# Four-layer graph network on one core: the last group's layers 2 and 3 in two pieces, activation tables loaded ahead, transposes between the last steps, and an order written out operation by operation

## The chip, the core and the metric

The kernel runs on one core of a Trainium2 chip. The engines named below are PE (TensorE, the matrix engine), DVE (VectorE), ACT (ScalarE), POOL (GpSimd) and SP (SyncE, which here only issues DMA transfers). Each engine works through its own list of instructions in the order in which the program put them; between engines, semaphores make an instruction wait until its inputs are there. The metric is the device time of one execution in microseconds (us), median of several runs. All data are float32.

## What is computed

The input is 128 small graphs of 64 nodes with 256 features each, and their adjacency matrices. Two graphs fill the 128 partitions, and such a pair is called a block, so there are 64 blocks. Four layers follow each other, each as `x = layernorm(x + layer(x))`:

```
# layer 0: five message-passing steps with a GRU cell
for l in range(5):
    agg = A^T @ (h @ weight[l]);  h = gru_cell(agg, h, w_ih, w_hh, b_ih, b_hh)
# layer 1: neighbour sum, 256 -> 1024 features, RMS norm, silu, 1024 -> 256
agg = eps * x + adj @ x;  h = silu(rmsnorm(agg @ W1 + b1) * rms_weight);  out = h @ W2 + b2
# layer 2: map to the tangent space, neighbour sum, back onto the ball
t = artanh(|x|) * x / |x|;  s = adj @ t;  out = project(tanh(|s|) * s / |s|)
# layer 3: attention over neighbours
h = x @ W_w^T + W_b;  u = adj * exp(e_i + f_j + a_b);  out = (u / sum(u)) @ h
```

A graph's rows never meet another graph's, so any set of blocks can be worked on alone.

## The kernel before, in words

The 64 blocks are cut into 16 groups of NB = 4 blocks (512 rows); `group(g)` (from L635) writes down all operations of one group, layers 0 to 3, as a *stream*. Layer 0 (`gated`, from L774) holds most of the matrix work. Layer 1's product into 1024 features is `by_sums` (the `p_ah`, `p_bh` and `p_ch` products of L1000, copied to `hid` by L334 or L335 and added up by L1005); the squares for the RMS norm are L986, their sum `ps_ss`, the factor `ps_rms`, the scaling L1049 and the silu L1051. The product back, `ps_o1` (32 matrix products of 256 columns for a group; the profile drops the digit and calls it `ps_o`), is the last large piece of matrix work of a group.

What follows is short work in a long chain, and it is done for the group's four blocks together. Sum onto the residual (L707), layer norm (`layer_norm`, L712 to L751: statistics L733 and L734 on DVE, a power on POOL L737, an offset L746, the scaled rows `x_n` by L339 on ACT or L340 on DVE), then layer 2: a row of tiny DVE operations on 128 x 4 values (L1090 to L1113), one of them a logarithm on ACT (L1098) and one a polynomial (`series`, L1101) that takes the logarithm's place where the norm is under `SERIES_BELOW`; the rows scaled (`tan`, L1117 or L1118), four products with the adjacency (`ps_sup`), squares with a sum on ACT (L1130), a square root on POOL (L1134), a tanh on ACT (L1139), six tiny DVE operations (`onto_ball`, L1142), the sum (L707) and a layer norm. Layer 3: eight transposes (`ps_T`, L668), copies to `x3T` (L334), eight products of 258 columns (`ps_a`), exponentials (L1189), scaled rows `hw` (L1192), four products with the adjacency (`ps_att`), a few tiny DVE operations (L1204 to L1207), the sum (L707), a layer norm and the output transfer (L1212).

Only the last two groups, 14 and 15, take this DVE form, the transposes by PE, and the statistics instructions (`summed` is false, `late` is true). The other fourteen do the tiny operations on POOL and the transposes by DVE and DMA.

ACT holds one set of function tables at a time. The logarithm, the silu and the exp are in three different sets (tanh is in the last two), and going from one to another takes an `ACT_TABLE_LOAD` in front of the function that needs it.

The order of the work on all engines is not the order in which the operations are written down. `Plan` (L54) goes through the streams with a cost model: at each step it takes, of the next few operations of each engine and up to four streams, the one that can start first, with ties settled by one of four rules; which rule holds in which stretch of 7 us is written in the string `CHOICES` (L156). It keeps eight PSUM banks, the DMA transfers and the ACT table in account. `issue` (L224) then gives out the operations in that order, and the order is kept on each engine.

```
    for g in range(NG):
        flow.stream()
        group(g)
    flow.issue()
```

Of the kernel before, what the change touches and what calls it, by code (L numbers as in the profile page):

```python
# [14 lines left out]
OP = mybir.AluOpType  # L15
# [7 lines left out]
SERIES_BELOW = 0.25  # L23
# [19 lines left out]
class Op:  # L43
    __slots__ = ("eng", "us", "run", "ways", "stream", "n", "kb", "sets", "need", "then", "bufs", "opens", "id", "way", "port")

    def __init__(self, ways, stream, n, kb, sets, port=()):
        self.port = port
        self.ways = {eng: (us, run) for eng, us, run in ways}
        self.eng, self.us, self.run = ways[0]
        self.stream, self.n, self.kb, self.sets = stream, n, kb, sets  # L50
        self.need, self.then, self.bufs, self.opens, self.id, self.way = 0, [], (), None, 0, 0.0


class Plan:  # L54


    def __init__(self, flow):
        self.flow = flow
        ops = [o for s in flow.streams for o in s]
        self.need = [o.need for o in ops]  # L60
        self.at = [0.0] * len(ops)
        self.uses = {}
        self.clock = dict.fromkeys(flow.AHEAD, 2.5)
        self.queues = [{e: deque(o for o in s if e in o.ways) for e in self.clock} for s in flow.streams]
        self.banks = [0.0] * BANKS
        self.left, self.first, self.bus = len(ops), 0, 0.0
        self.lands = [0.0] * flow.TRANSFERS
        self.order, self.table, self.port = [], None, 0.0

    def advance(self, until, rank):  # L70


        flow, need, at, clock, banks = self.flow, self.need, self.at, self.clock, self.banks
        while self.left and clock["PE"] < until:
            best = None
            for s in range(self.first, min(self.first + flow.WINDOW, len(self.queues))):
                for e, q in self.queues[s].items():
                    opened = False
                    for _, o in zip(range(flow.AHEAD[e]), q):
                        t = max(clock[e], at[o.id], self.port) if e in o.port else max(clock[e], at[o.id])  # L80
                        if o.opens is not None:
                            if opened or not banks or need[o.id]:
                                opened = True
                                continue
                            t = max(t, banks[0])
                        elif need[o.id]:
                            continue
                        elif o.kb and e != "POOL":
                            t = max(t, self.lands[0])
                        elif o.sets and self.table not in o.sets:  # L90
                            t += flow.TABLE
                        key = (t + flow.SOONER if len(o.ways) > 1 and e == "DVE" else t, *rank(s, o))
                        if best is None or key < best[0]:
                            best = key, o, e, t
            if best is None:
                return False
            _, o, eng, t = best
            if o.sets and self.table not in o.sets:
                self.table = o.sets[0]
            for e in o.ways:  # L100
                self.queues[o.stream][e].remove(o)
            self.order.append((eng, o))
            end = t + o.ways[eng][0]
            clock[eng] = end
            if eng in o.port:
                self.port = end
            if o.opens is not None:
                banks.pop(0)
            for b in o.bufs:
                n = self.uses.get(b, b.left) - 1  # L110
                self.uses[b] = n
                if not n:
                    banks.append(end + flow.hop(eng, "PE"))
                    banks.sort()
            if o.kb:
                self.bus = max(self.bus, end + flow.DMA[0]) + o.kb / flow.DMA[1]
                end = self.bus + flow.DMA[2]
                if o.eng != "POOL":
                    self.lands = [*self.lands[1:], end]
            for u in o.then:  # L120
                need[u.id] -= 1
                at[u.id] = max(at[u.id], end + flow.hop(eng, u.eng))
            self.left -= 1
            while self.first < len(self.queues) and not any(self.queues[self.first].values()):
                self.first += 1
        return True


class Flow:

    AHEAD = {"PE": 32, "DVE": 10, "ACT": 10, "POOL": 4, "SP": 2}


    HOPS = {"from PE": 0.22, "to PE": 0.42, "else": 0.06, "own": 0.0}

    REACH = {"from PE": 0.22, "to PE": 0.15, "else": 0.06, "own": 0.0}

    SOONER = 0.4


    DMA = (2.0, 330.0, 1.0)
    TRANSFERS = 8

    TABLE = 1.28
    WINDOW, STRETCH, LAGS = 4, 7.0, (60.0, 150.0)
    CHOICES = ("0010032202000010000101000000100101200211212021110210210022212000010021010211122100122212200010120021"  # L156
               "0210111100010100200111200121100102102211102100100010001002101010121001100100121112200201010102002100"
               "1010101001102000211100212100110100021110222020000101220210121200200010100201210100110111010011010111"
               "1000111101110110111001011000")
# [47 lines left out]
    def hop(self, e, to, hops=None):  # L207
        hops = hops or self.HOPS
        if e == to:
            return 0.0 if e == "PE" else hops["own"]  # L210
        return hops["from PE" if e == "PE" else "to PE" if to == "PE" else "else"]

    def ways(self):

        for i, o in enumerate(o for s in self.streams for o in s):
            o.id = i
        path = {}
        for ops in self.streams:
            longest = 0.0
            for o in reversed(ops):  # L220
                path[o] = o.us + max((path[u] + self.hop(o.eng, u.eng, self.REACH) for u in o.then if u.stream == o.stream), default=0.0)
                o.way = longest = max(longest, path[o])

    def issue(self):  # L224
        self.ways()
        ranks = (lambda s, o: (s, o.n), lambda s, o: (s if o.kb else -s, o.n), *(lambda s, o, lag=lag: (lag * s - o.way, s, o.n) for lag in self.LAGS))
        plan, until = Plan(self), 0.0
        for c in self.CHOICES:
            until += self.STRETCH
            assert plan.advance(until, ranks[int(c)])  # L230
        assert not plan.left
        last = {}
        for eng, o in plan.order:
            made = o.ways[eng][1]()
            for i in made if isinstance(made, list) else [made]:
                if eng in last:
                    self.tc.add_manual_dep(i.ins, last[eng].ins.name, self.BEHIND, reason="the plan's order")
                last[eng] = i
# [3 lines left out]
def kernel(  # L242
# [392 lines left out]
    def group(g):  # L635
        s = g % NF
        NB = SIZES[g]
# [74 lines left out]
        def layer_norm(y, st, tag, name, norm=None):  # L712
# [6 lines left out]
            def row(b):  # L719
                return [(y, b)]  # L720

            if summed:
                few_s((lambda: mv[:, :, 0], mv), lambda: st[:, :, 0], -1.0 / D, OP.mult, [st])
                for b in range(NB):
                    act(400, lambda b=b: nc.scalar.activation(
                        o[:, b, :], y[:, b, :], AF.Square, bias=mv[:, b, 0:1], accum_out=st[:, b, 1:2]),
# [4 lines left out]
            else:  # L731
                for b in range(NB):
                    dve(256, lambda b=b: nc.vector.bn_stats(st[:, b, :], y[:, b, :]), [(st, b)], row(b))  # L733
# [14 lines left out]
            for b in range(NB):  # L748
                scaled(256, lambda b=b: o[:, b, :], lambda b=b: y[:, b, :], lambda b=b: rstd[:, 0, b:b + 1],
# [3 lines left out]
        if g >= 2:  # L753
            load(g)
        xt, xs = loads.pop(g)
        ed = edge[s]
        ps = bank("ps_adjT")
        for b in range(NB):
            turn(lambda ps=ps, b=b: nc.tensor.transpose(ps[:, b * P:(b + 1) * P], ed[:, b, :], ident.tile()),
                 [ps], [ed])  # L760
        adjT = u("adjT", "adjT", (P, NB, P))
        copied(R, lambda: adjT.tile().rearrange("p b (m r) -> p b m r", m=Q),
               lambda ps=ps: ps[:, :R].rearrange("p (b r m) -> p b m r", b=NB, m=Q), [adjT], [ps])
        dve(R, lambda: nc.vector.tensor_scalar(ed[:, :NB, :], ed[:, :NB, :], 0.0, None, OP.not_equal), [ed], [ed])
        hT = u("h", "hT", (P, KD, R))
# [8 lines left out]
        def gated(l, h):  # L774
# [13 lines left out]
            def agg_of(n):  # L788
                aggregate(agg, hr, n, ed, l > 0)
# [460 lines left out]
```

## Time and profile before

| what | value |
|---|---|
| three runs | 2296.31, 2296.64 (median), 2298.32 us |
| the profiled execution: its own time | 2296.92 us |
| its span, first to last instruction | 2295.1 us |
| PE busy | 2245.7 us, 98% of the span |
| DVE, ACT, POOL busy | 1696.8 us (74%), 1308.8 us (57%), 554.3 us (24%) |
| mean granted PE clock | 0.994 of full speed |
| last `ps_o1` product of group 15 ends | 2252.08 us |
| last PE instruction ends | 2284.1 us |

Times inside the execution are counted from the first instruction. A float32 product runs on PE as two passes, so the profile counts two matmuls for each product that the kernel asks for; a transpose of 128 x 128 is one. "Idle" of an engine is the length of a stretch less its busy time in it.

### The profile page before, as it was taken

Reading aid. Unit: us, or ns where it says so; the run is one execution under the profiler, and the core shown is the slowest. Engines: PE = TensorE matmul, PEld = TensorE weight load, DVE = VectorE, ACT = ScalarE, POOL = GpSimd, SP = SyncE. Lnnn points to the kernel's source line nnn. Section 1 sums busy time; section 2 is a strip of 40 time slices with the busy share of each in tenths; the row PEclk is TensorE's granted clock in tenths of the full one; section 3 lists DMA queues with packets and bytes.
Section 4 is the critical chain, followed back from the end, with each engine's and each line's share of the span. In section 5 each row is a group of like instructions: output and inputs, shape, how many; then the busy total and the mean of one; then the engine's idle time right before and its main releaser. Section 6 shows DMA issues by size and latency. Waiting matters only on the chain.

```text
span 2295.1 us, 32440 instructions
## 1 busy us (share of the span) xinstructions
PE 2245.7 (98%) x11242; PEld 1979.1 (86%) x11242; DVE 1696.8 (74%) x3633; ACT 1308.8 (57%) x2800; POOL 554.3 (24%) x902
## 2 busy tenths in 40 slices
PE   9999999999999999999999999999999999999986
PEld 7888888888888888888888888888888888888774
DVE  5777867767777778677777777778777777777776
ACT  3344656675556556566566656556565665555564
POOL 2200222441122223132322223222231322112201
PEclk9999999999999999999999999999999999999998
DMA  5111112121212012121211212012122121211200
GB/s 146 33 23 33 28 19 58 19 49 29 48 28 47 22 28 58 19 45 33 36 42 25 52 28 47 21 29 49 28 49 37 22 53 21 49 19 20 46 10 19
DMA packets 428771, 84.21 MB, mean 37 GB/s; under 512 B 399124, under 2 KB 427824, under 8 KB 428608
## 3 DMA queue, kind: packets, MB, share of 16 engines
q1 hardware_dynamic: 426880, 80.26, 17.7%
q8 instruction: 89, 1.46, 0.3%
q10 hardware_dynamic: 1328, 1.31, 0.2%
q0 software_dynamic: 400, 0.57, 0.1%
q14 instruction: 74, 0.61, 0.1%
HBM read 32.55 MB, written 8.39 MB: 18 GB/s over the span
## 4 chain that ended last, share of the span: by engine, by line
PE 93%; DVE 3%; ACT 1%; POOL 1%; DMA 1%; issue 1%; SPq 0%; POOLq 0%; ACTq 0%; DVEq 0%
PE p_ga L817 23%; PE p_gc L817 12%; PE ps_o L316 9%; PE ps_agg L316 7%; PE p_ix L823 6%; PE p_gb L817 6%; PE p_hx L823 6%; PE p_ah L1000 4%; PE p_hy L823 4%; PE p_iy L823 4%; PE ps_a L316 2%; PE p_ch L1000 2%; PE ps_att L316 1%; PE ps_sup L316 1%; PE p_bh L1000 1%; PE ps_wmih L316 1%
## 5 line engine op out<-in xcount | busy, mean ns | idle before, releaser
L316 PE MATMUL ps_o<-w2s,hid 128*128 128x256 f32 x1024 | 230.9, 379 | 4.3 <-ACT hid L1051 4.3
L316 PEld LDWEIGHTS ps_o<-w2s,hid 128*128 128x128 f32 x1024 | 194.0, 190 | 31.7 <-ACT hid L1051 5.5
L351 POOL TENSOR_SCALAR mv<-st 128x4 f32<-128x4 f32 x56 | 15.6, 278 | 829.5 <-DVE y L707 442.0
L339 ACT ACTIVATE hnb<-p_hx,half_b 128x256 f32<-128x256 f32 x213 | 100.3, 471 | 143.0 <-PE p_hx L823 111.7
L817 PE MATMUL p_gc<-tA,w_h 128*128 128x256 f32 x640 | 173.2, 381 | 0.1
L817 PE MATMUL p_gc<-tB,w_a 128*128 128x256 f32 x640 | 172.3, 379 | 1.1 <-DVE tB L354 1.0
L817 PE MATMUL p_ga<-tA,w_h 128*128 128x256 f32 x640 | 171.7, 379 | 0.0
L817 PE MATMUL p_ga<-tB,w_a 128*128 128x256 f32 x640 | 168.4, 379 | 1.1 <-DVE tB L354 1.1
L817 PE MATMUL p_ga<-hT,w_h 128*128 128x256 f32 x640 | 168.3, 380 | 0.7 <-DVE U L867 0.4
L817 PE MATMUL p_ga<-agg,w_a 128*128 128x256 f32 x640 | 167.1, 379 | 0.0
L316 PEld LDWEIGHTS ps_agg<-edge,hr 128*128 128x128 f32 x1024 | 142.2, 193 | 12.4 <-DVE a_t L621 3.0
L316 PE MATMUL ps_agg<-edge,hr 128*128 128x128 f32 x1024 | 143.5, 276 | 2.8 <-DVE a_t L621 2.6
L870 ACT ACTIVATE U<-U,half_b 128x512 f32<-128x512 f32 (+1 forms) x160 | 94.0, 628 | 79.7 <-DVE U L867 79.6
L817 PEld LDWEIGHTS p_gc<-tB,w_a 128*128 128x128 f32 x640 | 121.0, 190 | 17.8 <-DVE tB L354 1.6
L817 PEld LDWEIGHTS p_ga<-tB,w_a 128*128 128x128 f32 x640 | 120.5, 190 | 18.1 <-DVE tB L354 1.8
L817 PEld LDWEIGHTS p_gc<-tA,w_h 128*128 128x128 f32 x640 | 121.2, 191 | 16.6 <-ACT V L334 0.5
L817 PEld LDWEIGHTS p_ga<-agg,w_a 128*128 128x128 f32 x640 | 119.7, 190 | 15.7 <-issue 0.5
L817 PEld LDWEIGHTS p_ga<-hT,w_h 128*128 128x128 f32 x640 | 118.5, 190 | 16.0 <-DVE U L867 0.8
L817 PEld LDWEIGHTS p_ga<-tA,w_h 128*128 128x128 f32 x640 | 117.9, 190 | 14.1
L334 ACT COPY agg<-ps_agg 128x512 f32<-128x512 f32 x140 | 81.0, 579 | 78.9 <-PE ps_agg L316 77.9
L870 ACT ACTIVATE V<-V,half_b 128x256 f32<-128x256 f32 (+1 forms) x160 | 87.8, 586 | 59.5 <-DVE V L867 58.9
L883 DVE TENSOR_TENSOR V<-p_ix,V 128x256 f32<-128x256 f32 x192 | 80.6, 420 | 35.3 <-PE p_ix L823 32.4
(285 smaller groups left out, 5667.1 us busy)
## 6 DMA issues: line engine op xcount, KB each, us to landing
hr<-t SPq DMA_DIRECT2D x256, 128.0 KB, 3.2
x<-in_x_dram SPq DMA_DIRECT2D x64, 128.0 KB, 2.7
xr<-in_x_dram SPq DMA_DIRECT2D x16, 512.0 KB, 4.3
out_dram<-x_n SPq DMA_DIRECT2D x16, 512.0 KB, 2.9
xs<-in_x_dram SPq DMA_DIRECT2D x120, 64.0 KB, 2.4
x3T<-t SPq DMA_DIRECT2D x56, 128.0 KB, 3.1
edge<-in_adj_dram SPq DMA_DIRECT2D x64, 32.0 KB, 2.2
wm<-in_L_gnn_weight_dram SPq DMA_DIRECT2D x5, 256.0 KB, 3.3
```

What stands on the lines that cost most here:

```text
L316: return nc.tensor.matmul(o, lhsT, rhs, start=(k == 0), stop=(k == nk - 1))
L334: flow.either([("ACT", 0.22 + 0.00077 * n, lambda: nc.scalar.copy(o(), i())), ("DVE", 0.145 + 0.00105 * n, lambda: nc.vector.tensor_copy(o ...
L339: flow.either([("ACT", 0.3 + 0.0008 * n, lambda: nc.scalar.activation(o(), i(), AF.Identity, bias=bias(), scale=scale())), ("DVE", 0.145 + ...
L351: pool(0.25, lambda: nc.gpsimd.tensor_scalar(w[0](), x(), s0, s1, op0, *((op1,) if op1 else ())), [w[1]], r)
L817: pe(HR, lambda i=i, w=w, c=c: nc.tensor.matmul(ps[:, c * HR:(c + 1) * HR], w[:, m, c * P:(c + 1) * P], v[i][0](), start=first and i == 1 ...
L823: pe(HR, lambda: nc.tensor.matmul(ps[:, j * HR:(j + 1) * HR], w[:, m, :], v[0](), start=first, stop=True, skip_group_check=True), [ps], [( ...
L870: act(HR if len(w) == 1 else R, lambda: nc.scalar.activation(o(), src(), AF.Tanh, bias=half_b[:, i * KD + c:i * KD + c + 1], scale=0.5), w ...
L883: dve(HR + 44, lambda: nc.vector.tensor_add(uu[:, c, half(n)], region(ps, j), uu[:, c, half(n)]), [(uu, (n, c))], [ps, (uu, (n, c))])
L1000: pe(HR, lambda c=c: nc.tensor.matmul(ps[:, c * HR:(c + 1) * HR], w1f[:, w, (2 * q + c) * P:(2 * q + c + 1) * P], v[0](), start=first and ...
```

## The change

1. **Last group in two pieces.** `group(g)` stops for g = 15 after layer 1 and returns `y1` and `adjT`. Two more streams then do layers 2 and 3 for two blocks each (`NB` = 2): piece 0 for blocks 0 and 1 in the buffers of slot 1, piece 1 for blocks 2 and 3 in those of slot 0. `layer_norm` gets the argument `at`, the first row block to read. Each piece has its own output transfer, so there are 611 transfers on SP's list for 610.
2. **Tables ahead.** In groups 14 and 15, `table` puts a one-operand `Ln` (before the chain of layer 2) and a one-operand `Tanh` (after it) on ACT. With this, ACT's list has six more small activations and 49 table loads for 47.
3. **Transposes between the steps.** In piece 1 only, `busy` puts 4 x 6 PE transposes into a bank that nobody reads, each six after one tiny result: `rn`, `n2`, `us` (shown as `ss`) and `urn` (shown as `rn`).
4. **Shorter polynomial.** `SERIES_BELOW` goes from 0.25 to 0.125, and the polynomial loses three of its seven terms, for all groups: 84 tiny POOL instructions less over groups 0 to 13, and three tiny DVE instructions less in each chain of groups 14 and 15.
5. **Order.** `Plan`, its cost model and `CHOICES` go. `placed` reads a string `ORDER` with one mark for each of the 13105 operations; a mark names the engine, the stream (of six) and the place in that engine's waiting list.

In the order that results, half of PE's products stand 10 or more places from where they stood, nine in ten within 43, counted among products of one kind and pair of tiles. On DVE, half stand 14 or more places away. The groups begin and end in the same sequence up to group 13. At the end it differs: before, the 32 `ps_o1` products of group 14 and the 32 of group 15 stand mixed together, and layer 2 of both groups stands behind them. After, group 14's `ps_o1` stand before group 15's first layer-1 product, and group 14's four `ps_sup` before group 15's `ps_o1`. Group 13's `ps_a` and `ps_att` stand among group 15's layer-1 products, where they stood about the start of group 15's fifth message-passing step. Behind group 15's last `ps_o1` stand group 14's `ps_T`, `ps_a` and `ps_att`, and the two pieces, piece 0 ahead of piece 1.

The core of the diff:

```
-SERIES_BELOW = 0.25
+SERIES_BELOW = 0.125
...
-    def issue(self):
-        self.ways()
...
-        for c in self.CHOICES:
-            until += self.STRETCH
-            assert plan.advance(until, ranks[int(c)])
...
+    def placed(self):
+        at, n = self.SIGNS.index, len(self.SIGNS)
+        waiting = [{e: [o for o in s if e in o.ways] for e in self.ENGINES} for s in self.streams]
+        first, marks = 0, iter(self.ORDER)
+        for c in marks:
+            i = at(next(marks)) * n + at(next(marks)) if c == "~" else at(c)
+            i, e = divmod(i, len(self.ENGINES))
+            i, s = divmod(i, self.AHEAD)
+            o, eng = waiting[first + s][self.ENGINES[e]][i], self.ENGINES[e]
...
+            yield eng, o
...
-    def group(g):
-        s = g % NF
-        NB = SIZES[g]
+    def group(g, piece=None):
+        s, NB, base = piece[:3] if piece else (g % NF, SIZES[g], 0)
...
+            if g == NG - 1:
+                return y1, adjT
+        else:
+            y1, adjT = piece[3:]
+            st1 = stats()
...
-        x2 = layer_norm(y1, st1, "A", "n1", xn)
+        x2 = layer_norm(y1, st1, "A", "n1", xn, base)
+        def table(func, sets, after):
+            if not summed:
+                act(4, lambda: nc.scalar.activation(warm, one4, func), [], [after], sets)
+        def busy(after, n=6):
+            if piece and base:
+                ps = bank("ps_warm")
+                for i in range(n):
+                    turn(lambda i=i: nc.tensor.transpose(
+                        ps[:, i % 4 * P:(i % 4 + 1) * P], after.tile()[:, :1].to_broadcast([P, P]), ident.tile()), [ps], [after])
+        table(AF.Ln, LN, xn)
...
+            busy(rn)
...
-                    v.scalar_tensor_tensor(ser.tile(), n2.tile(), 1.0 / 13.0, one4[:, :NB], OP.mult, OP.mult),
+                    v.scalar_tensor_tensor(ser.tile(), n2.tile(), 1.0 / 7.0, one4[:, :NB], OP.mult, OP.mult),
                     *(v.scalar_tensor_tensor(ser.tile(), ser.tile(), 1.0 / q, n2.tile(), OP.add, OP.mult)
-                      for q in (11, 9, 7, 5, 3)),
+                      for q in (5, 3)),
...
+            busy(n2)
...
+        table(AF.Tanh, TANH, fac)
...
+        busy(us)
...
+            busy(urn)
...
     for g in range(NG):
         flow.stream()
-        group(g)
+        made = group(g)
+        for i in range(2 if made else 0):
+            flow.stream()
+            group(g, ((g + 1 - i) % NF, SIZES[g] // 2, SIZES[g] // 2 * i, *made))
     flow.issue()
```

## The prediction

> **What bounds the kernel now.** I read the busy time by stretches first, then PE's waits near the end, then the chain of work that ended last, then PE's and ACT's instructions after the last `ps_o1`.
>
> The columns of the stretches are: from and to, length, busy time (instructions) of PE, PE's weight loads, DVE, ACT, POOL, then the granted PE clock, the DMA share and GB/s.
>
> ```profile
> 100.00:200.00 100.00, 100.00 (x512) 89.32 (x511) 77.70 (x150) 45.21 (x87) 0.00 (x0) 1.00 0.17 27
> 200.00:600.00 400.00, 395.94 (x1987) 350.55 (x1986) 294.75 (x623) 235.07 (x502) 104.15 (x176) 1.00 0.18 34
> 1400.00:1800.00 400.00, 399.44 (x2023) 355.06 (x2022) 304.59 (x637) 233.50 (x503) 102.23 (x164) 1.00 0.18 36
> ```
>
> ```profile
> 2100.00:2160.00 60.00, 55.95 (x275) 48.43 (x273) 44.55 (x90) 35.45 (x83) 18.58 (x42) 1.00 0.16 31
> 2160.00:2190.00 30.00, 28.82 (x138) 25.54 (x137) 19.67 (x57) 17.13 (x37) 5.16 (x6) 0.89 0.17 46
> 2190.00:2226.00 36.00, 28.53 (x136) 23.70 (x136) 30.54 (x58) 22.65 (x38) 4.39 (x3) 0.95 0.00 0
> 2226.00:2252.10 26.10, 26.07 (x127) 22.72 (x125) 14.27 (x49) 10.91 (x18) 2.64 (x2) 1.00 0.00 1
> 2252.10:2269.20 17.10, 5.61 (x16) 3.89 (x16) 12.14 (x60) 10.14 (x32) 4.62 (x4) 0.82 0.00 0
> 2269.20:2284.10 14.90, 14.86 (x64) 11.73 (x64) 11.66 (x42) 10.72 (x26) 2.68 (x2) 0.86 0.00 0
> 2284.10:2295.10 11.00, 0.02 (x1) 0.00 (x0) 5.16 (x21) 3.16 (x6) 1.19 (x2) 0.63 0.27 95
> ```
>
> From 100 to 2100 us PE is full: the idle of the stretches adds up to 7.5 us in 2000 (0 to 100 us has 6.7 more). No order can win more there than this idle. The end is another case: 12.7 us of idle from 2100 to 2252.1, then 43.0 us in which PE has some 20 us of work. PE's waits from 2100 us on name the causes (total, times, longest):
>
> ```profile
> PE ps_T L668 <- ACT x_n L339: 5.9, 1, 5.9
> PE ps_sup L316 <- DVE tan L1118: 5.3, 1, 5.3
> PE p_hy L823 <- DVE y L707: 3.7, 1, 3.7
> PE p_ah L1000 <- DVE hid L1005: 2.7, 1, 2.7
> ```
>
> And the PE and ACT instructions behind `ps_o1`, where the chain also runs:
>
> ```profile
> 2252.47 1.99 PE L316 MATMUL ps_sup<-tan,adjT 128*128 128x256 f32 x8 [0.41 <-ACT tan L1117]
> 2260.21 1.28 ACT L1139 ACT_TABLE_LOAD   x1
> 2269.24 2.16 PE L668 MATMUL ps_T<-ident,x_n 128*128 128x128 f32 x8 [5.90 <-ACT x_n L339]
> 2271.20 4.77 PE L316 MATMUL ps_a<-wattT,x3T 128*128 128x258 f32 x16
> 2277.11 1.12 PE L668 MATMUL ps_T<-ident,x_n 128*128 128x128 f32 x8
> 2278.69 3.69 PE L316 MATMUL ps_a<-wattT,x3T 128*128 128x258 f32 x16
> 2282.22 1.90 PE L316 MATMUL ps_att<-hw,adjT 128*128 128x257 f32 x8
> ```
>
> The first `ps_T` group takes 2.16 us, the second 1.12: the clock had fallen in the idle before the first. I call the end of the last `ps_o1` E (2252.1). Last PE work is at E + 32.0, the last `x_n` at E + 39.0 (2290.04 + 1.09 on ACT), the span's end at E + 43.0.
>
> **The sum, part by part.** Pitches, from the chain and the timeline after E: a product 0.432 us (two matmuls of 0.216), a transpose 0.14, a dependent tiny DVE operation 0.20, a sum L707 0.43, statistics of a block 0.53, a POOL power 1.01 + 0.1, `x_n` on ACT 0.61 then 0.48 each, a table load 1.28.
>
> *Up to E.* Of the 12.7 us, 4.9 are one event: group 13's last sums L707 stand ahead of group 15's transposes on DVE (`p_hy` 3.7 above, and `ps_hr` 1.2). In the new order these sums stand behind group 15's RMS factor, so the event goes. In their place 13 products of group 14's `ps_o1` (5.6 us) cover the layer norm of group 15 (2.9 us DVE, 1.1 POOL, 1.0 ACT and DVE: 5.0). What is late next is the norm of layer 1: after the last `p_ah` there is a copy and squares (3.2), sums (0.8), `ps_ss` (0.8), DVE and POOL (1.5), `ps_rms` (0.6), scaling and silu (1.4), some 8.5 us, against 4.8 us of PE work left beside it (four `ps_sup`, four `ps_att`, `ps_ss`, `ps_rms`): 3.7 idle. The eight scalings follow at 0.72 us, and the first products wait 1.3 for them. With 1 for small gaps, 6.0 of idle for 12.7: -6.7. Group 14's `ps_sup` (1.8) now come before E: +1.8. So E moves by -4.9, between -8 (idle 3) and 0 (the new chain as bare as `p_ah` and `ps_o1` were, 7.4, and small gaps as before).
>
> *Behind E.* I put the new order's DVE, ACT, POOL and PE lists side by side and let each operation begin at the later of its inputs and its engine. For piece 1, which ends last: sums, statistics, power, E + 2.8; then its tiny operations, shared on DVE with piece 0's and with group 14's 1.2 us bias sum, E + 6.6; logarithm 6.8; the table load behind it (both logarithms stand ahead of one load), 8.1; `tan` on DVE 8.5, its other half on ACT only at 11.0, behind group 14's `hw`; `ps_sup` and squares 11.9; root 13.0; the ball operations, behind 2.9 us of group 14's sums, 16.8; sums, statistics 18.9, power and offset 20.4; `x_n`, `ps_T`, copy 22.0; `ps_a`, `hw`, `ps_att` 25.1; sums and statistics of two blocks instead of four 27.9; power, offset, `x_n` 29.8. Before it was 39.0, so this sum alone gives -9.2. If the pieces don't overlap at all, only the last layer norm is shorter, by two blocks: 2 x (0.43 + 0.53) on DVE, two ratios, and one `x_n` less: -3. I take 31.5 (-7.5), a quarter of the way back, because DVE had 0.7 of the time busy here already and in such a list every meeting adds. The output transfer is 256 KB for 512: 4.0 us before, 3.8 taken: -0.2.
>
> *Tables.* The loads that count are the one behind the logarithms (in the sum) and two in group 15's squares (`Ln`, then `Exp` for group 13), which ACT pays beside group 13's `ps_a`; if that cover is gone, 2.6.
>
> *Transposes.* 24 x 0.14 = 3.4 us of PE (6.5 at the pitch of 0.27 of the first `ps_T`), in front of which PE waits for `rn`, `n2`, `us` and `urn`. Behind each wait stand `ps_a` of group 14, piece 1's `ps_sup`, group 14's last `ps_att`, and piece 0's `ps_T`; in my list each of these has its inputs later than the transposes' wait ends (E + 4.7, 6.7, 11.9, 15.4 against piece 1's `tan` at 8.5, `hw` at 12.3, `x_n` at 16.2), but for two `ps_a`. So 0, at worst 1.4 for two sixes that push. What they bring is the full clock for the pieces, which my pitches assume; without it a group's `ps_T` and `ps_a` cost 1.04 + 1.08 more, by the two pairs of rows above.
>
> The Trainium skill has a rule against this part: in "TensorE: Matmul & The Clock Gate", Part 4 on PE-mode transpose, it says that transposes do not count as PE activity for the clock as products do. The trace does not decide it: the clock was 0.50 while the first `ps_T` ran, but only for 2 us. By the rule the result would be some 2 us above my forecast.
>
> *Polynomial.* DVE: 3 x 0.2 = 0.6 us per chain, in the sum. POOL: 84 x 0.28 = 23 us on an engine busy 24% of the time, hidden by other groups' products: 0; at most 1.7 us per group if a group's chain were bare, and only group 13's is near that.
>
> *Order from 0 to 2100 us.* PE's work is the same. It can win at most the idle, 7.5, and 3.8 of the first 100 us (60 to 100). It can lose: if all 2000 us went as the worst stretch shown (4.06 in 400), 20.3 for 7.5, +12.8. The operations moved by tens of places, not hundreds, so the row it is nearest to is the old one: 0.
>
> Sum: -4.9 - 7.5 - 0.2 = -12.6 from the profiled execution's 2296.9, which is 0.3 above the median: **2284.3**, say 2284.5.
>
> **The rivals.** *(a) The pieces queue behind one another.* DVE's list mixes both pieces and group 14; one late input there holds all three. For it: DVE busy 12.1 of 17.1 us. Against: the chain's own waits (table load, powers, ACT) leave room. Then -4.9 - 3 - 0.2: 2288.8.
>
> *(b) The transposes don't hold the clock,* or come in the way: the forecast + 2.1 to 3.5: 2287.
>
> *(c) The body gives it back.* The new order is tighter or looser everywhere; if it runs like the worst stretch, +12.8 takes the gain: 2294 to 2298. Against: the first 2000 us lie within one place of the old distances for many products.
>
> *(d) Slower: products just behind DVE.* In each of 80 GRU steps the products of the sums `tA` and `tB` wait for DVE; the trace has this wait twice only:
>
> ```profile
> PE p_ga L817 <- DVE tB L354: 1.1, 1, 1.1
> PE p_gc L817 <- DVE tB L354: 1.0, 1, 1.0
> ```
>
> Moved products that now stand directly behind their sums would pay up to 1.1 each time. From 12.6 / 80 = 0.16 us per step on, it decides; at 0.25 the time is 2304.
>
> *(e) That the change doesn't do what it says* is only open for the transposes, which is (b).
>
> **How the numbers follow.** Forecast 0.62, (a) 0.16, (b) 0.08, (c) 0.08, (d) 0.06. The measurement tells 0.2% from nothing, 4.6 us: faster means below 2292.0, which forecast, (a) and (b) are: 0.86. (c) is the same: 0.08. (d) slower: 0.06. The range takes E between -8 and 0, the part behind E between -9.4 and -3, some us of the body: 2277 below, and above it reaches into (c), 2293.
>
> **What would show it.** Right: E near 2247; idle in the 36 us before the last `ps_o1` about 5, with `ps_o1` waiting for `hid`; no `p_hy` wait for L707; last PE work near E + 26; last `x_n` between E + 30 and E + 33; one table load there; idle from 100 to 2100 us near 8. Wrong: idle above 15 in the body, spread over waits for `tA`, `tB` or `hid`; the clock near 0.5 between the pieces' steps; piece 0's `x_n` not ahead of piece 1's by 4 us or more.

## The result, and the profile after

| | before | after |
|---|---|---|
| median of the runs | 2296.61 us (4 runs, 2296.31 to 2298.32) | 2285.31 us (4 runs, 2283.73 to 2286.30) |
| profiled execution, its span | 2296.92, 2295.1 us | 2285.90, 2284.1 us |
| mean granted PE clock | 0.994 | 0.998 |
| E, end of the last `ps_o1` | 2252.1 us | 2250.9 us |
| from E to the end of the span | 43.0 us | 33.2 us |

The ratio of the times is 0.9947, with a 95% interval from 0.9932 to 0.9963. The medians are 11.3 us apart, where 12.1 were predicted. The sum was right and its parts were not, as the stretches show first. The columns are those of the stretches before: from and to, length, busy time (instructions) of PE, PE's weight loads, DVE, ACT and POOL, then the granted PE clock, DMA share, GB/s.

```profile
30.00:40.00 10.00, 6.94 (x21) 4.25 (x20) 2.12 (x5) 1.27 (x5) 4.70 (x8) 0.83 0.77 185
100.00:200.00 100.00, 99.99 (x485) 86.16 (x484) 78.17 (x154) 42.49 (x88) 11.07 (x15) 1.00 0.14 25
200.00:600.00 400.00, 395.50 (x1988) 346.10 (x1987) 309.39 (x643) 236.43 (x513) 101.17 (x163) 1.00 0.19 37
1400.00:1800.00 400.00, 397.56 (x2008) 351.65 (x2008) 302.05 (x632) 232.22 (x501) 95.51 (x150) 1.00 0.19 37
2100.00:2160.00 60.00, 60.00 (x305) 53.39 (x304) 43.73 (x95) 34.08 (x67) 11.34 (x21) 1.00 0.08 18
2160.00:2190.00 30.00, 29.99 (x152) 26.10 (x151) 26.38 (x52) 23.76 (x51) 7.90 (x18) 1.00 0.11 18
2190.00:2226.00 36.00, 35.10 (x171) 29.70 (x170) 30.83 (x71) 21.70 (x39) 7.33 (x4) 1.00 0.14 31
2226.00:2250.90 24.90, 21.89 (x100) 16.72 (x98) 20.72 (x72) 20.09 (x49) 5.70 (x8) 1.00 0.07 22
2250.90:2266.80 15.90, 12.41 (x65) 9.05 (x64) 14.05 (x74) 12.69 (x38) 3.07 (x4) 1.00 0.00 0
2266.80:2276.10 9.30, 8.50 (x34) 4.87 (x32) 8.10 (x34) 6.74 (x17) 2.40 (x3) 1.00 0.01 2
2276.10:2284.10 8.00, 0.02 (x1) 0.00 (x0) 3.18 (x13) 2.82 (x6) 0.70 (x1) 0.77 0.39 131
```

The end got better than forecast: from 2100 us to E PE is idle for 3.9 us (12.7 before), at full clock (0.89 and 0.95 before). But E hardly moved, by 1.2 us. The gain was spent on the way: the stretch from 1400 to 1800 us has 2.44 us of idle for 0.56, all of 100 to 2100 us has 12.3 for 7.5, and at 30 to 40 us there is a hole of 3.1 us with a lower clock behind it, which the kernel before didn't have. The same stretch of the kernel before, and the wait that makes the hole in the changed kernel:

```profile
30.00:40.00 10.00, 10.00 (x41) 6.69 (x40) 3.44 (x9) 2.41 (x7) 7.20 (x14) 1.00 0.75 157
```

```profile
PE ps_wmT L616 <- DMA wm<-in_L_gnn_weight_dram: 3.1, 1, 3.1
```

PE's waits from 2100 us on (total, times, longest) no longer name the sums of group 13 (`p_hy` 3.7 and `ps_hr` 1.2 before); no wait there is longer than 1.6 us. `ps_warm` is the bank of the transposes that nobody reads; the other lines are among the longest waits of real products:

```profile
PE ps_warm L1149 <- DVE off L812: 1.6, 1, 1.6
PE ps_T L734 <- ACT x_n L406: 1.4, 3, 0.5
PE ps_o L383 <- ACT hid L1118: 0.9, 2, 0.7
PE ps_sup L383 <- DVE tan L1206: 0.9, 1, 0.9
```

And the instructions behind E:

```profile
2252.40 1.15 PE L734 MATMUL ps_T<-ident,x_n 128*128 128x128 f32 x6 [0.54 <-ACT x_n L406]
2257.93 1.28 ACT L1279 ACT_TABLE_LOAD   x1
2266.18 1.09 ACT L406 ACTIVATE x_n<-y,off,rstd 128x256 f32<-128x256 f32 x2 [0.32 <-DVE off L812]
2267.74 2.01 PE L383 MATMUL ps_a<-wattT,x3T 128*128 128x258 f32 x8
2271.00 1.09 ACT L406 ACTIVATE x_n<-y,off,rstd 128x256 f32<-128x256 f32 x2 [0.44 <-DVE off L812]
2275.42 0.70 PE L383 MATMUL ps_att<-hw,adjT 128*128 128x257 f32 x2 [0.17 <-ACT hw L1282]
2279.01 1.59 ACT L406 ACTIVATE x_n<-y,off,rstd 128x256 f32<-128x256 f32 x3 [1.68 <-DVE off L812]
```

Piece 0's `x_n` (2266.18) is 4.8 us ahead of piece 1's (2271.00): the pieces do overlap. Last PE work ends at E + 25.2, the last `x_n` at E + 29.7 (before E + 32.0 and E + 39.0).

**A count that idle time does not give.** With the starts of all matmuls in the trace one can add up what each should take when nothing waits. This is its pitch, the time from its start to the next one's: 0.2163 us for 256 columns, in proportion for others, 0.109 at least. In the kernel before, 9,491 of 9,555 neighbours between 100 and 2000 us keep that pitch within 0.02 us. Time passed less this sum is the time lost to waits and to the clock. By stages of work (the sum of the pitches, so "0 to 50 us of work" ends where the matmuls so far should have taken 50 us):

| lost, us | before | after |
|---|---|---|
| 0 to 50 us of work | 5.5 | 10.4 |
| 50 to 100 | 4.2 | 0.0 |
| 100 to 1990 | 11.0 | 20.6 |
| 1990 to E | 21.9 | 8.7 |
| work up to E | 2209.5 | 2211.2 |
| behind E | 43.0 | 33.2 |

The differences, +4.9, -4.2, +9.6, -13.2, +1.7 (group 14's `ps_sup`) and -9.8, add up to -11.0, the difference of the spans. From 100 to 2000 us only 6.7 and 11.6 us of this is shown as idle. The rest hides in "busy": a matmul is shown for 0.38 us and the next could start after 0.22, so a wait of up to 0.16 leaves no gap. Steps that are 0.02 to 0.30 us too long occur 40 times before (3.8 us) and 78 times after (8.0 us), longer ones 9 times (7.9 us) and 16 times (13.7 us).

### The profile page after: what moved, and what is told of

The parts are those of the page before. It is cut to its first block, busy times and chain, and to the rows that moved or that the text cites. A ratio compares the mean times of both kernels' runs of the same rounds, so it can differ in the third digit from the quotient of the medians.

```text
span 2284.1 us, 32381 instructions
## 1 busy us (share of the span) xinstructions
PE 2250.0 (99%) x11266; PEld 1970.5 (86%) x11266; DVE 1718.0 (75%) x3671; ACT 1305.5 (57%) x2798; POOL 521.0 (23%) x822
## 4 chain that ended last, share of the span: by engine, by line
PE 91%; DVE 5%; SPq 1%; DMA 1%; ACT 1%; issue 1%; POOL 0%; ACTq 0%; DVEq 0%; POOLq 0%
PE p_ga L884 23%; PE p_gc L884 11%; PE ps_o L383 9%; PE ps_agg L383 7%; PE p_gb L884 6%; PE p_ix L890 6%; PE p_hx L890 6%; PE p_ah L1067 5%; PE p_iy L890 4%; PE p_hy L890 4%; PE p_ch L1067 2%; PE ps_a L383 2%; PE p_bh L1067 1%; PE ps_sup L383 1%; PE ps_att L383 1%; PE ps_wmih L383 1%
## 5 line engine op out<-in xcount | busy, mean ns | idle before, releaser
L884 PE MATMUL p_ga<-hT,w_h 128*128 128x256 f32 x640 | 174.4, 381 | 1.9 <-DVE U L934 1.6
L884 PE MATMUL p_ga<-agg,w_a 128*128 128x256 f32 x640 | 171.8, 380 | 0.0
L383 PEld LDWEIGHTS ps_agg<-edge,hr 128*128 128x128 f32 x1024 | 148.5, 191 | 12.1 <-DVE U L950 0.5
L383 PE MATMUL ps_agg<-edge,hr 128*128 128x128 f32 x1024 | 150.5, 275 | 0.2
L424 POOL TENSOR_TENSOR sqt<-sqt,sqh 128x512 f32<-128x512 f32 x56 | 74.8, 1335 | 150.2 <-ACT sqh L1053 86.0
```

The lines of the kernel that those rows point to most:

```text
L383: return nc.tensor.matmul(o, lhsT, rhs, start=(k == 0), stop=(k == nk - 1))
L424: pool(0.24 + 0.00211 * n, lambda: nc.gpsimd.tensor_tensor(o(), x0(), x1(), op), w, r)
L884: pe(HR, lambda i=i, w=w, c=c: nc.tensor.matmul(ps[:, c * HR:(c + 1) * HR], w[:, m, c * P:(c + 1) * P], v[i][0](), start=first and i == 1 ...
```

## The experiments

Every median stands beside runs of the kernel before on the same chip (medians of these from 2297.5 to 2298.1), and the ratio is to those. "Order" is the long string of places; a diff of it is given as lists in words. The *body* is all of PE's work up to 1990 us, the *end* the rest, the *head* the beginning of the body; a *seam* is the place where the lists of two orders are joined.

**1 and 2. The body of one order with the end of the other.**

```diff
-ORDER: the changed kernel's places
+ORDER: e1: before's places up to 1990 us of PE work, then the changed kernel's
+       e2: the changed kernel's up to 1990 us, then before's (group 15 unsplit,
+           no one-element Ln and Tanh, no transposes)
```

> The changed kernel with its first 1990 us of TensorE work put back into the order of the kernel before (on every engine and the DMA queue), the rest as changed. Theory (the new order lost in the body what it won before E): idle of TensorE from 0 to 2100 us falls from 17.9 to about 14.2 us, the drop of the granted clock at 30 to 40 us is gone (about 1.5 us), so E, the end of the last ps_o1, goes from 2250.9 to about 2246 and the time from 2285.3 to about 2280. Rival (the changed end needs the changed body before it: what is saved in the body comes back as idle between 2000 us and E): 2284 to 2286.

> The reverse: the first 1990 us of TensorE work in the order of the changed kernel, then the kernel before's own end: group 15 unsplit, no table loads ahead, no transposes (the short polynomial stays). Theory (body of the new order is looser): slower than the kernel before by what the body loses, 3.7 of idle and 1.5 of clock: about 2301.5, end of ps_o1 near 2257. Rival (the body costs nothing, the loss stands elsewhere): 2296 to 2297.5; below 2296 if the short polynomial gives something on the path.

Measured (median, ratio, its 95% interval): e1 2276.34 us, 0.9909 [0.9895, 0.9922]; e2 2306.29 us, 1.0035 [1.0021, 1.0049]. Both theories held in sign and both sizes were too small. The four corners:

| ratio to before (median, us) | end of before | changed end |
|---|---|---|
| body of before | 1 | 0.9909 (2276.34) |
| changed body | 1.0035 (2306.29) | 0.9947 (2285.31) |

With either end the changed body costs 0.35 to 0.38%, 8.0 to 8.7 us of 2297; with either body the changed end brings 0.88 to 0.91%, 20.2 to 20.9 us. Each ratio is known to about 3 us either way, so the signs are clear and the sizes are rough. The short polynomial is in e1 and e2 alike and not in the kernel before; e1's body, with it, lost 20.2 us for 20.7. In e1 E is at 2239.1 and the span ends 33.0 later; in e2 E is at 2263.9 and the span ends 43.2 later. The losses of e2 in the same stages are 32.3 up to 1990 us, 22.1 to E. Three stretches of e1, which has the small idle of the body of before and no idle in the end:

```profile
30.00:40.00 10.00, 10.00 (x41) 6.76 (x40) 3.44 (x8) 2.42 (x7) 7.31 (x13) 1.00 0.70 154
1400.00:1800.00 400.00, 399.45 (x2020) 355.02 (x2019) 305.76 (x637) 233.38 (x502) 98.85 (x152) 1.00 0.18 36
2160.00:2190.00 30.00, 30.00 (x155) 26.33 (x154) 26.28 (x53) 22.95 (x43) 6.82 (x14) 1.00 0.06 19
```

Two stretches of e2, where idle and low clock of the old end are back:

```profile
2160.00:2190.00 30.00, 24.78 (x116) 20.53 (x115) 23.37 (x62) 14.47 (x35) 5.16 (x6) 0.94 0.15 32
2190.00:2220.00 30.00, 26.10 (x132) 22.63 (x131) 24.70 (x51) 15.70 (x29) 3.39 (x2) 0.94 0.07 22
```

and two of e2's PE waits, the old ones of the sums and of `hid`:

```profile
PE p_hy L889 <- DVE y L772: 3.7, 1, 3.7
PE p_ah L1066 <- DVE hid L1071: 3.6, 2, 2.7
```

**3. Without the transposes.**

```diff
-            if piece and base:
+            if False:
```

> The changed kernel without the 24 transposes behind rn, n2, us and urn of group 15's second piece; everything else in the same order. Theory 1 (they hold the clock): the granted clock falls behind E as it did before (0.8 to 0.9 in the stretch, ps_T and ps_a at double pitch), the time rises by about 2.1 us to 2287.4. Theory 2 (transposes do not count as activity for the clock, by the rule of the Trainium skill, or the pieces' own products hold it): clock and time as in the changed kernel, 2285.3, or 0.5 to 1.4 less because four waits in front of the transposes go.

Measured: 2285.75 us, 0.9949 [0.9936, 0.9961]: the same time. The clock did fall without them. Two stretches that begin 13 us behind E, of the changed kernel and of e3, and then e3's `ps_a` of piece 0, which took 2.01 us with the transposes:

```profile
2264.00:2274.00 10.00, 7.73 (x38) 5.00 (x37) 9.30 (x41) 5.62 (x14) 2.08 (x3) 1.00 0.00 1
```

```profile
2262.00:2272.00 10.00, 7.22 (x21) 4.74 (x20) 7.70 (x35) 4.54 (x12) 1.20 (x3) 0.66 0.00 1
```

```profile
2266.11 3.81 PE L383 MATMUL ps_a<-wattT,x3T 128*128 128x258 f32 x8
```

From E to the end of the span it took 34.9 us for 33.2, 1.7 more, but e3's E happened to be 1.9 earlier. Of this, 1.6 were lost in the first 50 us of work (10.4 and 8.8). The place is seen at 34 us, where both wait for `wm` (3.1 and 2.7 us): the three microseconds behind that wait ran at 0.59 in the one execution (first line, changed kernel) and at 1.00 in the other:

```profile
34.00:37.00 3.00, 3.00 (x11) 2.44 (x12) 0.98 (x2) 0.28 (x1) 0.45 (x1) 0.59 0.77 120
```

```profile
34.00:37.00 3.00, 2.92 (x14) 2.29 (x15) 1.27 (x3) 0.55 (x2) 0.90 (x3) 1.00 0.81 128
```

**4. The wm loads ahead.** `wm` are the weights of the message-passing steps, `w1f` and `w2s` those of layer 1, which are needed later.

```diff
 DMA queue, from 19 us on
+wm (fourth), wm (fifth)
 w1f, w2s, x, aw, w1f, w2s, edge, edge, x, x
-wm (fourth)
 x
-wm (fifth)
```

> The changed kernel with one edit: on the DMA queue the two late loads of wm stand ahead of those of w1f and w2s instead of behind them. Theory (the wait of ps_wmT for wm at 34 us, 3.1 us, and the dropped clock behind it are a plain loss that everything after inherits): 3 to 4.5 us less, about 2281.5. Rival (TensorE then waits for the next late load or for DVE, or the later w1f and w2s make another wait): 2284.5 to 2285.5.

Measured: 2281.55 us, 0.9931 [0.9918, 0.9943], 3.8 less than the changed kernel, as the first theory said. The hole is gone (30 to 40 us: PE busy 10.00 at clock 1.00), no new wait took its place, and E came 5.2 earlier than in the profiled execution of the changed kernel.

**5 to 8. Joining the good parts, and the parts of the end.** The head of e4, the body of before and the changed end; then the same without transposes, without the one-element `Ln` and `Tanh`, and with group 15 in one piece.

```diff
 ORDER of e5
+e4's places up to 134 us of PE work, before's up to 1990, then the changed kernel's
 e6:
-            if piece and base:
+            if False:
 e7:
-            if not summed:
+            if False:
 e8:
-            if g == NG - 1:
-                return y1, adjT
```

> Three parts joined: the changed kernel's first 134 us of TensorE work with the two wm loads ahead, then the order of the kernel before up to 1990 us of work, then the changed end. Theory (losses of separate stages add up): of the body_before run (2276.3) the idle in its first 100 us (6.3 us against 2.6 in wm_ahead) goes, 2272 to 2273, last ps_o1 near 2235. Rival (at the seam the lists of two orders meet and TensorE waits there): 2274 to 2277.

> The joined kernel without the 24 transposes. In the first run without them the medians were the same (2285.75 and 2285.31), but the profile had the granted clock down for the last ps_T and ps_a, and last TensorE work at E + 26.9 instead of E + 25.2; there the start of the kernel scattered. Theory 1 (they hold the clock and are worth what the profile says): 1.7 us above the joined kernel. Theory 2 (what they hold isn't on the chain, or they cost what they bring): within 0.5 of it.

> The joined kernel without the six one-element Ln and Tanh activations. Theory (loads ahead of the logarithm and of the root's tanh lie in ACT's idle time, without them they lie in the chain of the last piece): 1.3 us more for one load on the chain, 2.6 for two. Rival (the other piece's work covers them, or the logarithm needs its load in any case): within 0.5 of the joined kernel.

> The joined kernel with group 15's layers 2 and 3 in one piece (no transposes; table loads ahead stay); the work up to about the last ps_o1 stands in the same order, what follows is put in a new order for four blocks, with group 14's ps_T and ps_a ahead of group 15's ps_sup. Theory (the pieces shorten the chain behind E because one piece works while the other waits): E as in the joined kernel, last TensorE work at E + 30 to 33, the time 7 to 10 us above it. Rival (the order was the gain and not the pieces): at most 3 us above it.

Measured: e5 2286.84 us (0.9955 [0.9943, 0.9968]), e6 2286.06, e7 2287.87, e8 2293.96 (0.9987 [0.9978, 0.9995]).

e5 missed by 14 us, and beyond its rival. From 0 to 134 us of work it is about as good as e4 (6.2 and 5.1 us lost), but between 100 and 200 us of work it loses 15.6 us. A stretch of e5, and PE's longest wait in it:

```profile
100.00:200.00 100.00, 91.82 (x424) 74.59 (x422) 78.13 (x150) 37.14 (x78) 10.66 (x15) 1.00 0.17 29
```

```profile
PE p_hx L886 <- ACT hnb L402: 4.4, 1, 4.4
```

At 134 us of work the two orders do not hold the same operations: by the planner's costs, operations of 17.1 us of PE and 16.5 us of DVE stand before the seam in one list and behind it in the other. At 1990, where e1 joins, it is 0.4 and 1.4. A seam there cost nothing (20.7 us lost up to 1990 in before, 20.2 in e1).

e6 against e5: E to the end 33.9 us for 33.2, medians 0.8 apart the other way. Nothing that the time shows.

e7: the table load now stands behind E, on the way to piece 0's logarithm, and `ps_sup` waits for `tan`, which it did not in e5. From the timelines of ACT and of PE in e7:

```profile
2254.31 1.28 ACT L1180 ACT_TABLE_LOAD   x1
```

```profile
2256.64 1.13 PE L379 MATMUL ps_sup<-tan,adjT 128*128 128x256 f32 x4 [0.89 <-DVE tan L1202]
```

From E to the end it took 36.7 us for 33.2. Not all of these 3.5 us are the load's 1.28: piece 0's `ps_a` took 3.81 us for 2.01, so the clock had fallen too. The medians differ by 1.0, the runs by up to 4.4 among themselves. One load on the chain is shown by the profile; its price in time (1.3 expected) is not settled.

e8: E is where e5 has it (2252.6 and 2252.0), E to the end took 39.4 us for 33.2, the median is 7.1 higher, as the theory said. PE waits once for each step of the one chain:

```profile
2261.05 1.99 PE L379 MATMUL ps_sup<-tan,adjT 128*128 128x256 f32 x8 [1.93 <-ACT tan L1199]
2266.24 3.60 PE L379 MATMUL ps_att<-hw,adjT 128*128 128x257 f32 x8 [3.20 <-ACT hw L1276]
2272.95 2.17 PE L730 MATMUL ps_T<-ident,x_n 128*128 128x128 f32 x8 [3.10 <-ACT x_n L402]
```

So of the 9.8 us won behind E some 6.2 are the pieces', as far as this pair tells: e8 also lacks the transposes (0.7 in e6's profile), and behind E it has an order of its own, written for one piece; a better one was not tried. The other 3.6 (43.0 to 39.4) came with what e8 shares with the changed end, such as the order, in which group 14's `ps_T` and `ps_a` stand ahead of group 15's `ps_sup`; they were not taken apart.

**9 to 11. A closer seam; again without transposes; the long polynomial.**

```diff
 ORDER of e9
-e4's places up to 134 us of PE work, before's up to 1990, then the changed kernel's
+e4's places up to 348 us of PE work, before's up to 1990, then the changed kernel's
 e10: as e6
 e11:
-SERIES_BELOW = 0.125
+SERIES_BELOW = 0.25
...
-            for q in (3, 1):
+            for q in (9, 7, 5, 3, 1):
... (likewise the coefficients in front of it, and the DVE form)
```

> The joined kernel with its first seam at 348 us of TensorE work instead of 134. There the two orders hold nearly the same set of operations: 0.4 us of TensorE work and 0 of VectorE on the one side only, against 17.1 and 16.5 at 134, and 0.4 and 1.4 at the second seam, 1990. Theory (a seam costs by how far the two lists are apart there; losses of stages add up otherwise): the body_before run lost 10.4 us to waits up to this place, wm_ahead 5.4, so 2276.3 - 5.0 = 2271.3, last ps_o1 near 2234. Rival (any seam of two orders costs, the one at 1990 was luck): 2278 or more.

> That kernel without the 24 transposes. Two earlier pairs gave +0.4 and -0.8 us in the medians, with starts that scatter by 3 us, while the profiles had last TensorE work 1.7 and 0.7 us later behind E and slow ps_a in the last 20 us. Theory 1 (the transposes hold the clock, part of that lies on the chain): 0.7 to 1.7 us above the kernel with them. Theory 2 (nothing on the chain): within 0.3 of it, with the clock down all the same.

> That kernel with the long polynomial of the kernel before in all groups (84 more POOL operations, three more VectorE operations in each chain of the last two groups). The prediction's terms: POOL 23 us in all, hidden, 0; VectorE 0.6 us for each chain behind E, of which piece 1's and a part of piece 0's lie on the path: 0.6 to 1.2 us above the joined_close run. Rival (POOL is on the path of some groups): 3 us or more above it.

Measured: e9 2275.81 us (0.9901 [0.9887, 0.9916]), e10 2275.81, e11 2278.12 (0.9910 [0.9895, 0.9924]).

e9 is 11.0 better than e5 and no better than e1; it lies between its theory (2271.3) and its rival (2278). It had lost 6.1 us at 300 us of work (e1 10.4), but 15.5 at 600 (e1 14.1): 4.3 us won ahead of the seam, 5.7 given back behind it. Of these 5.7, 4.2 lie at the seam, around one wait of PE, shown first. ACT's timeline says why, and two stretches show the clock behind it (all of e9; `hnb` on ACT is the copy of the GRU's product `p_hx` that must be made before the next product goes there):

```profile
358.04 0.70 PE L887 MATMUL p_hx<-tA,w_hn 128*128 128x256 f32 x2 [1.94 <-ACT hnb L403]
```

```profile
356.05 1.58 ACT L403 ACTIVATE x_n<-y,off,rstd 128x256 f32<-128x256 f32 x3 [1.71 <-POOL off L411]
357.54 0.45 ACT L403 ACTIVATE hnb<-p_hx,half_b 128x256 f32<-128x256 f32 x1
```

```profile
350.00:360.00 10.00, 8.06 (x41) 6.73 (x40) 6.97 (x19) 6.76 (x18) 3.06 (x5) 0.97 0.08 15
360.00:370.00 10.00, 10.00 (x46) 8.54 (x45) 7.91 (x16) 4.83 (x11) 0.97 (x1) 0.86 0.48 104
```

`hnb` needs `p_hx`, done by 353.1, and ACT idles 1.71 us from 354.3 on; but `hnb` stands behind three `x_n` of another group that wait for POOL. At the seam the layer norm of one order and the next step of the other had come to stand next to each other. Most of the rest, 1.3, came behind a wait that e1 has too: `ps_o1` waits 2.2 us for `hid` near 470 us, and the 24 matmuls behind it took 7.13 us in e9 and 5.45 in e1. The clock was 0.83 from 470 to 480 us in e9; no run shows why it fell in this one and not in e1.

e10: the third pair that the medians can't tell apart, E to the end 34.8 us for 34.0. In e9 itself the transposes failed to hold the clock (its `ps_a` took 3.51 us).

e11: 2.3 us more in the median, between theory and rival, though the runs overlap (2275.56 to 2278.55, e9 2274.36 to 2276.79). POOL is busy 24.8 us longer up to 2190 us, and PE is idle 4.7 us from 400 to 1000 us for 3.7. So the shorter polynomial may be worth something in the body too, about 1 us by one profile each; the runs don't settle it.

**12. Four operations moved at the seam.**

```diff
 ACT:  +hnb(p_hx)  x_n x_n x_n  -hnb(p_hx)  agg
 DVE:  +V +V +hnb(p_hy)  x_n t t  -V -V -hnb(p_hy)
```

> The joined_close kernel saved 4.2 us of waits in its first 100 us and gave it back between 300 and 600 us. At its first seam p_hx waits 1.94 us for hnb, whose copy on ACT stands behind the three x_n of group 0's second layer norm (they wait 1.71 for POOL's off); on VectorE the two sums V and the sum hnb stand behind x_n and its transposes (2.06 for off). The edit moves these four operations ahead of the x_n, on those two lists alone; all four have their inputs while their engine idles. Theory (that list order is the seam's cost: the wait, and the clock of 0.86 and 0.97 in the 20 us after it, 5.2 us together): 2272 to 2274, TensorE full from 350 to 360 us at clock 1.00. Rival (both orders' heads and bodies are only good with their own neighbours; the next late operation takes the wait's place): 2275 to 2277.

Measured: 2273.38 us (2272.92 to 2274.28), ratio 0.9896 [0.9879, 0.9912]. The same two stretches in e12:

```profile
350.00:360.00 10.00, 9.26 (x49) 7.95 (x48) 7.51 (x21) 7.45 (x20) 3.22 (x5) 1.00 0.07 14
360.00:370.00 10.00, 8.97 (x47) 7.37 (x47) 9.12 (x20) 4.93 (x13) 0.80 (x1) 1.00 0.47 103
```

The wait of 1.94 us for `hnb` is gone and the clock is full. Smaller waits took part of its place (`ps_hr` for `hT` 0.8, `p_ga` for `agg` 0.7), so PE is not full from 350 to 360 us, against what was expected, but the 20 us hold 96 matmuls for e9's 87. The lost time at 600 us of work is 12.4 for 15.5 and E comes 3.3 us earlier in the profiles; the medians differ by 2.4, with intervals of the ratios that overlap. Only a part of that is the edit's: at the seam the loss fell from 4.2 to 2.5 us, and 1.3 us more were saved behind the wait of `ps_o1` for `hid` near 470 us, where the 24 matmuls took 5.45 us this time. So list order is shown as a cost of the seam, for 1.7 of its 4.2 us; 2.5 stay with the smaller waits. This kernel has the lowest median of all: it is 24.6 us below the runs of before beside it, the changed kernel 11.3 below its own.

## Why the prediction was right, point by point

The forecast of 2284.5 us and its range held, but by luck: the body was taken as free and cost 8 to 10 us, and the end was taken as worth 12.6 and brought about 20; the two errors nearly cancelled. The signs that the prediction named show it only in part. E came at 2250.9 ("near 2247") and the body's idle was 12.3 us ("near 8"). The last `x_n` at E + 29.7 was a little ahead of its range, and the last PE work, the `p_hy` wait and the one table load were as said. None of its signs of being wrong appeared, since the loss in the body stayed under the 15 us of idle that would have told.

- **"Order from 0 to 2100 us ... the row it is nearest to is the old one: 0"** is the step that failed. It cost 8.0 to 8.7 us (the four corners), 10.3 by the lost time up to 1990 us in the profiles. Two reasons. The sum priced the body by the idle shown, and that was wrong: less than two thirds of the loss is shown as idle. And the first 100 us were taken as a chance to win 3.8, without a look at the DMA queue's list, where two of five `wm` loads had gone behind four loads of `w1f` and `w2s`; e4 prices that at 3.8 us. The wait of 50 to 100 us of work did go (4.2 to 0.0). What is left of the body's loss, 9.6 us from 100 us on, is spread over many waits, the longest of 1.5 us; e1 and e2 show that it goes with the order of these places. Which of its moves cause it stays open. Rival (c) named the mechanism and its price of 12.8, and gave it too small a chance; it took for granted that the end would gain no more than 12.6.
- **Up to E: -4.9** was mis-sized. In e1, where the body is the old one, E comes 13.0 earlier than before. The event named (sums of group 13 in front of group 15's transposes) went as said, `ps_o1` waits for `hid` as said, and idle from 2190 us to E was 3.9 for "about 5". From the last `p_ah` to the first `ps_o1` it took 8.4 us for the 8.5 of the sum, but more of it was covered: the waits in it are 0.9, 0.4, 0.8 and 0.7, 2.8 for 3.7, and the next wait is 0.2 for 1.3. Above all, the sum counted idle alone: before, the clock and the short waits cost another 8.4 us from 1990 us of work to E (21.9 lost, 13.5 idle). In the change that is 4.1 (8.7 lost, 4.6 idle).
- **Behind E: -7.5.** The hand-made sum gave 29.8 to the last `x_n`; it came at 29.7. The "quarter of the way back" that was added for meetings of the lists was the mistake. The trace has one table load there, as said, and it ends at E + 8.3 for 8.1. The output transfer took 3.5 us for 3.8.
- **Rival (a)**, pieces in a queue: no. Piece 0 is 4.8 us ahead of piece 1, and one piece in their place (e8) took 6.2 us longer behind E and 7.1 in the median.
- **Tables:** the one behind E and the two beside group 13's `ps_a` (at 2222.6 and 2225.0 us) are where the prediction had them. It doesn't mention that one more stands under the last `ps_o1` (2247.6 us), where it costs nothing; without the one-element operations that one moves behind E (e7).
- **Transposes: 0 of cost, the clock as gain.** No cost shows: piece 0's `ps_T` begins at E + 15.9 with them and without (the changed kernel and e3, e5 and e6). They do hold the clock in most runs: piece 0's `ps_a` took 2.01 us in six of eight profiles with them (the changed kernel, e1, e4, e5, e11, e12; 3.81 in e7, 3.51 in e9), and 3.81, 2.98 and 3.04 in the three with two pieces and without them (e3, e6, e10). But what they hold is worth 0.7 to 1.7 us from E on, not 2.1, and three pairs of medians (+0.4, -0.8, 0.0) cannot tell it from nothing. The Trainium skill's rule ("TensorE: Matmul & The Clock Gate", Part 4 on PE-mode transpose: transposes don't count as PE activity as products do) doesn't agree with these rows, six of eight against none of three, and the rows decide here.
- **Polynomial:** "POOL hidden: 0" may be about 1 us, by one profile of e11; this isn't shown beyond the scatter, and 0.6 per chain cannot be told apart from it.
- **Rival (d)** at its price of 0.25 us in each GRU step: no; `tB` is waited for twice, 2.5 us. As a kind it was there, as one of the body's many waits.

## What to carry to other kernels

Price a new order by the lost time, not by idle: add up the pitches of the matmuls and subtract; a wait under the difference between a matmul's shown length and its pitch (0.16 us here) is invisible in "busy". The Trainium skill ("Perfetto Trace Analysis", Identifying the Most-Contended Engine) says that matmul busy time is a bad measure of closeness to the limit; here PE's busy share rose from 98 to 99% while the body's loss doubled. Of the measures that it offers instead, the weight loads' busy share is 86% in both.

When a change has a part with a clear gain (here the end) and a reordering of everything else, measure the four corners; each half of the new order may be good or bad for itself, and the sum hides it. Two orders can be joined, but at a place where they hold the same operations: of the three seams here, the one that was 17 us of work apart lost 15.6 us, the two that were 0.4 apart 4.2 and nothing. And what then stands next to each other on ACT's and DVE's lists needs a look: an operation whose inputs are there should not stand behind one that waits for POOL.

## What had not been expected of the hardware

A wait can cost more than its length. Behind the 1.94 us wait of e9 the clock was 0.86 for 10 us, and 4.2 us were lost there in all; behind 3.1 us at the start of the changed kernel it was 0.59 for 3 us, behind 2.7 us in the same place of e3 it stayed 1.00. Near 470 us a wait of 2.2 us left the clock at 0.83 for 10 us in e9, and at 1.00 in e12. So the length of a wait alone did not say whether the clock fell. The runs of the changed kernel lie 2.6 us apart; that such waits are the reason is likely from e3, but not shown.
